# Masked graph attention, two layers: the score products in 32x64 tiles of TensorE in place of 32x128

## The chip, the cores and the metric

The kernel runs on one core of a Trainium2 chip. The metric is the device time of one execution in microseconds (us). Lower is better. Matrix products run on TensorE (PE in the profile), which first loads a stationary operand (its weights, PEld in the profile) and then streams a moving operand through the array; results land in PSUM and are read by VectorE (DVE), ScalarE (ACT)[...].

## What is computed

Sixteen graphs of 1024 nodes with 256 features each, float32, with an adjacency matrix per graph. Two layers follow each other; both have the form x + layer(relu(layernorm(x)), adj). The change lies in the first layer's attention:

```python
normed = layer_norm(x, gamma1, beta1)
qkv    = normed.reshape(b_, n_, H, HD).transpose(0, 2, 1, 3)      # H = 8 heads of HD = 32
scores = jnp.einsum('bhqd,bhkd->bhqk', qkv, qkv) * scale
masked = jnp.where(adj_matrix[:, None, :, :] > 0, scores, -jnp.inf)
attn   = jax.nn.softmax(masked, axis=-1)
out    = jnp.einsum('bhqk,bhkd->bhqd', attn, qkv)
x = x + out.transpose(0, 2, 1, 3).reshape(b_, n_, d_)
y = layer_norm(x, gamma2, beta2)
return x + gelu(y @ W1 + b1) @ W2 + b2
```

Queries, keys and values are the same array. The second layer is one graph attention head over 256 features, with logits from h a_12 h^T, leaky relu, the same mask, softmax and an output projection.

## The kernel before, in words

The program holds two versions of the computation; a small test at its start picks one, and with these inputs `fast_path` runs. All of what follows is there.

**Tiles.** For each graph `b`, `va` holds the normalized rows (128 nodes on the partitions, 256 features), and `kT` the same transposed: two groups `g` of four heads, each head on 32 partitions, 1024 nodes in the free dimension. Attention is done in 512 units, one for each graph (16), half of the queries (`qh`, 512 wide), group of four heads (`g`) and tile of 128 keys (`kt`).

**One unit.** `scores` makes the products of four heads, each with its 128 keys as the stationary operand (32 partitions by 128 columns) and its 512 queries as the moving one. Head `j` of a group uses the partitions `32 j` to `32 j + 31`, so the four products lie in four row groups of the array. They go to two PSUM tiles `sc0` and `sc1` of two heads each, a bank for a head (the name in the profile is `s`). The DVE adds the mask (L971), the ACT takes the exponential (L974), and one unit later `weigh` multiplies the result `e` with the values (L987, tile `o`): four products of 128 partitions by 32 columns, side by side in the four column groups. For graph 0 alone (`by_pe`), the mask of the first two heads is added on TensorE ahead of the score products by a product of the mask with an identity matrix.

**The rest of TensorE's work.** All other products (L570: the first layer's MLP `ph` and `po`, the second layer's `lg`, `pa`, `pg`, `pf`, `puT`) go through the helper `matmul`, which splits a product of 128 columns in four of 32 columns. Transposes are 128 by 128. Each float32 product stands in the profile as two weight loads and two matmuls: the 2048 score products of the program are 4096 records at L950. They are called its two passes below.

**Order.** The order of instructions on each engine is fixed by the program: six streams (attention, the previous graph's MLP and second layer, preparation, prologue, masks, setup) are merged by places written out by hand, with a `clock` that tells deferred pieces when they are due. The attention of one graph is interleaved with the remaining layers of the graph before it: between two units' products lie some 4 us of L570 products. At the end a dependency from each instruction to the one before it on its engine fixes the order for good.

Of the kernel before, what the change touches and what calls it, by code (L numbers as in the profile page):

```python
# [16 lines left out]
P = 128  # L17
# [476 lines left out]
def fast_path(  # L494
# [28 lines left out]
    nc = tc.nc  # L523
# [41 lines left out]
    def matmul(out, lhsT, rhs, start=True, stop=True):  # L565
        if not quarters[0]:
            nc.tensor.matmul(out, lhsT, rhs, start=start, stop=stop)  # L567
            return
        for c in range(0, P, HD):
            nc.tensor.matmul(out[c : c + HD], lhsT[:, c : c + HD], rhs, start=start, stop=stop)  # L570
# [165 lines left out]
    def defer(us, f):  # L736
        deferred.append((clock[0] + us, len(deferred), f))

        return clock[0] + us
# [145 lines left out]
    def make_turns():  # L885
        room = 3 - open_sums[0] - bool(summed) if open_sums[0] else 100
        while turns and turns[0][0] <= room:
            n, f = turns.pop(0)
            room -= n
            f()  # L890
# [40 lines left out]
    def attention(b, st):  # L931
        va, kT = st["va"], st["kT"]


        def scores(qh, g, kt):
            qs = slice(qh * QW, (qh + 1) * QW)
            sc = [
                psc.tile([P, 2, QW], F32, tag=f"sc{i}", name=f"s_{b}_{g}_{qh}_{kt}_{i}") for i in range(2)
            ]

            by_pe = 2 if b == 0 else 0
            if by_pe:
                for j in range(by_pe):
                    matmul(
                        sc[j // 2][:, j % 2, :], ident8, st[qh][:, kt // 2, :, kt % 2], start=True, stop=False
                    )
                clock[0] += 0.45
            for j in range(GH):
                r = slice(j * HD, (j + 1) * HD)
                nc.tensor.matmul(  # L950
                    sc[j // 2][:, j % 2, :],
                    kT[r, g, kt * P : (kt + 1) * P],
                    kT[r, g, qs],
                    start=j >= by_pe,
                    stop=True,
                )
            mb = st[qh][:, kt // 2, :, kt % 2].unsqueeze(1).to_broadcast([P, 2, QW])
            es = []
            if b == 0 and kt % 2:

                odd = midp.tile([P, 2, 2, QW], F32, tag="mid", name=f"odd_{g}_{qh}_{kt}")
            for i in range(2):
                if b == 0 and kt % 2:
                    e = odd[:, i]
                elif kt == 0:
                    e = accp.tile([P, 2, QW], F32, tag=f"acc{i}", name=f"acc_{b}_{g}_{qh}_{i}")
                else:
                    e = ep.tile([P, 2, QW], F32, tag="e", name=f"e_{b}_{g}_{qh}_{kt}_{i}")
                masked = sc[i]
                if 2 * i >= by_pe:  # L970
                    nc.vector.tensor_tensor(e, masked, mb, op=ALU.add)  # L971
                    masked = e
                es.append(e)
                weights = lambda e=e, masked=masked: nc.scalar.activation(e, masked, AF.Exp, scale=SCALE)  # L974
                if i == 0:
                    weights()
            return es, weights

        acc = {}


        def weigh(qh, g, kt, es):
            if kt == 0:
                acc[g, qh] = pso.tile([P, QW], F32, tag="o", name=f"o_{b}_{g}_{qh}")
            o = acc[g, qh]
            for j in range(GH):
                nc.tensor.matmul(  # L987
                    o[j * HD : (j + 1) * HD, :],
                    va[:, kt, (g * GH + j) * HD : (g * GH + j + 1) * HD],
                    es[j // 2][:, j % 2, :],  # L990
                    start=(kt == 0),
                    stop=(kt == NT - 1),
                )
            if b == 0 and kt % 2:

                if kt > 1:
                    for n, (e, w) in enumerate(zip(es, odds[g, qh])):
                        defer(1.0 + 2.5 * n, lambda e=e, w=w: nc.vector.tensor_add(e, e, w))
                odds[g, qh] = es
            if kt == NT - 1:  # L1000
                c = tmpp.tile([P, QW], F32, tag="w2", bufs=3, name=f"os_{b}_{g}_{qh}")
                nc.vector.tensor_copy(c, o)
                weighed.append((b, qh, g, c, [s[g, qh] for s in (sums, odds) if s]))

        sums, odds = {}, {}


        def add_up(qh, g, kt, e, i):
            if b == 0 and kt % 2:
                return  # L1010
            nc.gpsimd.dma_start(sums[g, qh][i], e, accum_op=ALU.add)  # L1011

        units = [(qh, g, kt) for qh in range(NQH) for g in range(NG) for kt in range(NT)]
        for u in units:
            make_turns()
            es, rest_of_weights = scores(*u)
            go_on()
            rest_of_weights()
            qh, g, kt = u
            if kt == 0:  # L1020
                sums[g, qh] = es
            else:
                for i in range(2):
                    defer(2.0 + 1.5 * i, lambda u=u, e=es[i], i=i: add_up(*u, e, i))
            scored.append((weigh, (*u, es)))
            yield

    def go_on():
        was_weighed, was_summed, was_totalled = weighed[:], summed[:], totalled[:]
        for l in (weighed, summed, totalled):  # L1030
            l.clear()
        if scored:
            f, args = scored.pop()
            f(*args)
        summed.extend(was_weighed)
        for args in was_summed:
            total(*args)
        for args in was_totalled:
            turns.append((2, lambda args=args: finish(*args)))
        clock[0] += 2.0  # L1040
# [351 lines left out]
    def stream_a():  # L1392
        for b in range(B):
            yield from spread(attention(b, states[b]), 32, b, b + 1)
        yield from spread(close_attention(), 4, B, B + .1)
# [146 lines left out]
```

## Time and profile before

| | |
|---|---|
| median of 3 runs | 3503.76 us (3500.55 to 3506.12) |
| profiled execution | 3501.46 us, of which the span is 3499.6 us |
| TensorE clock granted | 0.998 |
| PE busy | 3445.0 us (98% of the span), 46590 matmuls |
| PE weight loads | 1673.9 us, 46590 loads, beside the matmuls |
| DVE busy | 2758.3 us (79%) |
| ACT busy | 1857.8 us (53%) |
| POOL busy | 1412.8 us (40%) |
| score products (L950) | 592.5 us of PE busy time, 4096 matmuls |
| value products (L987) | 549.2 us in three groups, 4096 matmuls |

The profile comes from one execution, followed by the hardware profiler. A group of instructions is a row with the source line, the engine, the operation, the tile written and the tiles read, the shape, the count, the busy time and the mean duration of one. A duration of a matmul is its own from start to a modelled end; matmuls overlap, so the busy time of a group is far less than count times mean. A timeline row merges consecutive instructions of one group, with the start of the first and the time from it to the end of the last.

### The profile page before, as it was taken

To read this page: it belongs to the slowest core of one execution; us is meant where nothing else is said; L and a number is where in the kernel's file an instruction comes from. 1 tells how busy PE (TensorE), PEld (TensorE's weight loads), DVE (VectorE), ACT (ScalarE), POOL (GpSimd) and SP (SyncE) were. 2 spreads that over 40 slices of the span, in tenths; PEclk is the share of its full clock that TensorE was granted. 3 is DMA by queue.
4 is the path that set the end of the run, shared out by engine and by line. 5 is a ranking of instruction groups with operands and counts; after the bars stand their busy time and mean duration, and the time that the engine had idled before them with its cause. 6 is when DMAs were issued, how large, how long until landed. Compare 5 with 4: busy or idle time off the path is not lost.

```text
span 3499.6 us, 107320 instructions
## 1 busy us (share of the span) xinstructions
PE 3445.0 (98%) x46590; PEld 1673.9 (48%) x46590; DVE 2758.3 (79%) x5193; ACT 1857.8 (53%) x2184; POOL 1412.8 (40%) x1708
## 2 busy tenths in 40 slices
PE   6999999999999999999999999999999999999998
PEld 2244444444444444444444444444444444444477
DVE  6878788787877878888787888878878777887754
ACT  4555555555555555555555555555555555555522
POOL 3444443434434344343444534344344443434220
PEclk9999999999999999999999999999999999999999
DMA  7798889999899998989989899998989989899720
GB/s 183 147 182 173 181 164 185 182 186 188 161 187 176 191 184 165 181 167 190 195 167 183 165 185 185 177 190 164 186 177 191 183 165 179 171 191 182 147 63 14
DMA packets 281860, 597.81 MB, mean 171 GB/s; under 512 B 94882, under 2 KB 130084, under 8 KB 281380
## 3 DMA queue, kind: packets, MB, share of 16 engines
q0 software_dynamic: 124416, 453.04, 70.1%
q1 hardware_dynamic: 154276, 134.41, 15.5%
q8 instruction: 368, 6.03, 0.7%
q10 hardware_dynamic: 2688, 3.41, 0.3%
q14 instruction: 112, 0.92, 0.1%
HBM read 104.21 MB, written 16.78 MB: 35 GB/s over the span
## 4 chain that ended last, share of the span: by engine, by line
PE 94%; DVE 3%; DMA 1%; issue 1%; ACT 0%; POOL 0%; ACTq 0%; SPq 0%; DVEq 0%; POOLq 0%
PE s L950 15%; PE o L987 13%; PE pa L570 12%; PE po L570 12%; PE ph L570 12%; PE lg L570 10%; PE pg L570 3%; PE pf L570 3%; PE puT L570 3%; PE den L901 2%; PE ptf L1193 1%; PE pty L1117 1%; PE ptk L801 1%; PE ptos L922 1%; PE pa L567 1%
## 5 line engine op out<-in xcount | busy, mean ns | idle before, releaser
L974 ACT ACTIVATE e<-e 128x1024 f32<-128x1024 f32 x852 | 896.0, 1057 | 964.3 <-DVE e L971 728.3
L1011 POOL DMA_DIRECT2D acc<-e x864 | 754.9, 890 | 1438.3 <-DMA acc<-e 637.3
L971 DVE TENSOR_TENSOR e<-s,mk 128x1024 f32<-128x1024 f32 x852 | 1002.6, 1217 | 181.2 <-PE s L950 155.4
L950 PE MATMUL s<-kT 32*128 32x512 f32 x4096 | 592.5, 643 | 3.5 <-DVE odd L971 2.7
L987 PE MATMUL o<-e,va 128*32 128x512 f32 x3456 | 461.8, 605 | 2.1 <-ACT e L974 2.1
L570 PE MATMUL pa<-gw,e 128*32 128x258 f32 x7648 | 453.0, 380 | 0.0
L570 PE MATMUL lg<-fT,uT 128*32 128x256 f32 x7680 | 447.3, 379 | 0.0
L570 PE MATMUL ph<-yT,w 128*32 128x256 f32 x7808 | 446.5, 379 | 0.0
L570 PE MATMUL po<-w,hid 128*32 128x256 f32 x7680 | 439.3, 379 | 0.0
L570 PEld LDWEIGHTS ph<-yT,w 128*32 128x32 f32 x7808 | 255.3, 110 | 211.8 <-issue 51.1
L570 PEld LDWEIGHTS po<-w,hid 128*32 128x32 f32 x7680 | 250.3, 110 | 208.8 <-issue 58.3
L570 PEld LDWEIGHTS pa<-gw,e 128*32 128x32 f32 x7648 | 248.4, 110 | 212.0 <-issue 56.5
L570 PEld LDWEIGHTS lg<-fT,uT 128*32 128x32 f32 x7680 | 249.6, 110 | 209.0 <-issue 43.4
L1241 DVE SCALAR_TENSOR_TENSOR e<-lg,gw,mk 128x256 f32<-128x256 f32 x512 | 223.2, 477 | 72.0 <-PE lg L570 61.5
L1247 ACT ACTIVATE e<-e,shift 128x512 f32<-128x512 f32 x256 | 183.1, 717 | 181.6 <-DVE e L1246 116.0
L1144 DVE TENSOR_TENSOR hid<-ph,b1c 128x512 f32<-128x512 f32 x256 | 175.8, 687 | 91.6 <-PE ph L570 80.1
L950 PEld LDWEIGHTS s<-kT 32*128 32x128 f32 x4096 | 162.7, 184 | 163.8 <-issue 112.0
L987 PEld LDWEIGHTS o<-e,va 128*32 128x32 f32 x3456 | 68.6, 108 | 330.3 <-issue 187.3
L974 ACT ACTIVATE acc<-acc 128x1024 f32<-128x1024 f32 x124 | 131.1, 1057 | 132.9 <-DVE acc L971 128.4
L1246 DVE SCALAR_TENSOR_TENSOR e<-e 128x512 f32<-128x512 f32 x256 | 193.1, 754 | 8.8
L971 DVE TENSOR_TENSOR acc<-s,mk 128x1024 f32<-128x1024 f32 x124 | 146.1, 1218 | 20.2 <-PE s L950 19.8
L793 POOL TENSOR_TENSOR nrm<-nrm,g 128x256 f32<-128x256 f32 x128 | 112.9, 882 | 63.8 <-DVE nrm L727 63.8
(145 smaller groups left out, 3820.9 us busy)
## 6 DMA issues: line engine op xcount, KB each, us to landing
acc<-e POOLq DMA_DIRECT2D x864, 512.0 KB, 6.1
adj<-in_adj_dram SPq DMA_DIRECT2D x248, 256.0 KB, 5.6
h<-in_x_dram SPq DMA_DIRECT2D x64, 256.0 KB, 6.1
xb<-in_x_dram SPq DMA_DIRECT2D x128, 128.0 KB, 4.3
out_dram<-z SPq DMA_DIRECT2D x128, 128.0 KB, 4.0
adj<-in_adj_dram SPq DMA_DIRECT2D x4, 512.0 KB, 6.8
mk<-mq SPq DMA_TRANSPOSE x128, 6.5
w<-in_L_gnn_W_dram ACTq DMA_DIRECT2D x2, 1024.0 KB
```

What stands on the lines that cost most here:

```text
L570: nc.tensor.matmul(out[c : c + HD], lhsT[:, c : c + HD], rhs, start=start, stop=stop)
L793: nc.gpsimd.tensor_mul(nrm, nrm, g1)
L901: nc.tensor.matmul(den[j * HD : (j + 1) * HD, :], ones, acc[j // 2][:, j % 2, :], start=acc is accs[0], stop=acc is accs[-1],)
L950: nc.tensor.matmul(sc[j // 2][:, j % 2, :], kT[r, g, kt * P : (kt + 1) * P], kT[r, g, qs], start=j >= by_pe, stop=True,)
L971: nc.vector.tensor_tensor(e, masked, mb, op=ALU.add)
L974: weights = lambda e=e, masked=masked: nc.scalar.activation(e, masked, AF.Exp, scale=SCALE)
L987: nc.tensor.matmul(o[j * HD : (j + 1) * HD, :], va[:, kt, (g * GH + j) * HD : (g * GH + j + 1) * HD], es[j // 2][:, j % 2, :], start=(kt = ...
L1011: nc.gpsimd.dma_start(sums[g, qh][i], e, accum_op=ALU.add)
L1144: nc.vector.tensor_tensor(hid[:, f0 : f0 + 2, :], ph, b1c[:, f0 : f0 + 2].unsqueeze(2).to_broadcast([P, 2, CW]), op=ALU.add,)
L1241: nc.vector.scalar_tensor_tensor(e[:, j, :], lg[:, j, :], gw[:, kt, D : D + 1], st[c // 2][:, kt // 2, qs, kt % 2], op0=ALU.add, op1=ALU.add,)
L1246: nc.vector.scalar_tensor_tensor(e, e, ALPHA, e, op0=ALU.mult, op1=ALU.max)
L1247: ready = defer(2.5, lambda: nc.scalar.activation(e, e, AF.Exp, bias=shift))
```

## The change

The product of a head is split in two: its first 64 keys, then its last 64 keys, each against the same 512 queries. The stationary operand of one is 32 partitions by 64 columns, its result lies on 64 partitions of the same PSUM bank, and a unit has eight products where it had four. What reads the scores is not changed, nor is the order of anything else, and the planner's `clock` is not moved by it.

```diff
@@ scores @@
             for j in range(GH):
                 r = slice(j * HD, (j + 1) * HD)
-                nc.tensor.matmul(
-                    sc[j // 2][:, j % 2, :],
-                    kT[r, g, kt * P : (kt + 1) * P],
-                    kT[r, g, qs],
-                    start=j >= by_pe,
-                    stop=True,
-                )
+                for c in range(0, P, P // 2):
+                    nc.tensor.matmul(
+                        sc[j // 2][c : c + P // 2, j % 2, :],
+                        kT[r, g, kt * P + c : kt * P + c + P // 2],
+                        kT[r, g, qs],
+                        start=j >= by_pe,
+                        stop=True,
+                    )
```

## The prediction

> **What bounds the kernel now.** I read the shares of the engines first, then the chain that ended last, then one unit of attention in the timeline.
>
> ```profile
> PE 3445.0 (98%) x46590; PEld 1673.9 (48%) x46590; DVE 2758.3 (79%) x5193; ACT 1857.8 (53%) x2184; POOL 1412.8 (40%) x1708
> ...
> PE 94%; DVE 3%; DMA 1%; issue 1%; ACT 0%; POOL 0%; ACTq 0%; SPq 0%; DVEq 0%; POOLq 0%
> ...
> L950 PE MATMUL s<-kT 32*128 32x512 f32 x4096 | 592.5, 643 | 3.5 <-DVE odd L971 2.7
> L987 PE MATMUL o<-e,va 128*32 128x512 f32 x3456 | 461.8, 605 | 2.1 <-ACT e L974 2.1
> ...
> L950 PEld LDWEIGHTS s<-kT 32*128 32x128 f32 x4096 | 162.7, 184 | 163.8 <-issue 112.0
> L987 PEld LDWEIGHTS o<-e,va 128*32 128x32 f32 x3456 | 68.6, 108 | 330.3 <-issue 187.3
> ```
>
> TensorE is the bound: busy for 98%, 94% of the chain, and before the 4096 score matmuls idle for 3.5 us in all. By stretch, from 240 to 3300 us it idles for less than 4 us in 3060. So whatever a score unit takes on TensorE goes into the end time one to one, and a faster reader of the scores is worth nothing. "Busy" hides the loss, though: value products have the same count per unit as score products, the same 512 moving columns, and take less. The timeline of one unit shows why (start, us, engine, group, count; each line is from a window narrow enough to hold that step alone):
>
> ```profile
> 1004.21 0.40 PE L570 MATMUL ph<-yT,w 128*32 128x256 f32 x4
> ...
> 1004.54 0.20 PEld L950 LDWEIGHTS s<-kT 32*128 32x128 f32 x4 [0.41 <-DVE e L1241]
> ...
> 1004.54 0.71 PE L950 MATMUL s<-kT 32*128 32x512 f32 x4
> ...
> 1004.64 0.20 PEld L950 LDWEIGHTS s<-kT 32*128 32x128 f32 x4
> ...
> 1005.07 0.61 PE L950 MATMUL s<-kT 32*128 32x512 f32 x4
> ...
> 1005.61 0.16 PEld L987 LDWEIGHTS o<-e,va 128*32 128x32 f32 x8 [0.76 <-issue]
> ...
> 1006.06 0.61 PE L987 MATMUL o<-e,va 128*32 128x512 f32 x4
> ```
>
> Four score matmuls start together, one for each head's first pass, and 0.53 us later the four of the second pass. Between the two passes of `o` it is 0.45 us, and from the second pass of `o` to the next `ph` (first start 1006.49) 0.43. So a pass of 512 columns streams in 427 ns (2 x 213 of `ph`, whose passes of 256 columns follow each other at 215), whether it has 32 rows or 128. The rest is transition. The starts of single instructions, which the trace holds in ns, split it (they repeat in nearly all of the 512 units to within 2 ns):
>
> - `ph`'s last matmul starts 20 ns after its first and streams for 213; the score loads start 93 ns after that. This is the drain at the switch from 128x32 tiles to 32x128.
> - The first score matmul is recorded 1 ns after its load, but streams only from 107 ns later: its duration is 692 where the second pass has 587, and the loads of the second pass start 108 ns after the first ones. So 105 ns is **weight load with nothing to hide it**, because the array was drained.
> - The four starts are 7 ns apart, 20 ns from first to fourth. The last score start is followed by the load of `o` after 517 ns: 427 of streaming and 90 of drain.
> - `o`'s own first load lies bare for 25 ns (617 against 592).
>
> A unit of score and value products is thus 4 x 427 = 1708 ns of streaming and (93 + 105 + 20) + (90 + 25 + 20) = 353 ns of transition, 2.06 us, as the timeline has it.
>
> **What the Trainium skill says.** "TensorE: Matmul & The Clock Gate", section "LDWEIGHTS (loading the stationary operand)", prices a load by its columns alone, P / 1.2 ns: 107 for 128 and 27 for 32. The trace agrees with both (105 and 25). Its "Part 3: Packing small matmuls" says that row and column tiles compose and that a further tile adds about 4 ns; here a float32 tile, being two pairs of load and matmul, adds 7. The same part says that a load overlaps a running matmul only in another row group; the trace differs, since the second loads of `o` start at 1005.63, all on the same 128 rows, while its first pass streams. "TensorEngine Tiling (Array Packing)", section "Tiling Modes", lists 32x64 with eight tiles, and under "Key Properties" has a change of mode drain the engine: the 90 to 95 ns above.
>
> **The change, part by part.**
>
> 1. *Streaming.* Each pass has eight tiles of 32x64 where it had four of 32x128. If the eight run side by side, a pass stays at 427 ns. No row of before has this shape. Its neighbours do: four row tiles run together (L950), and four column tiles on the same rows run together (L987), so the same partitions can feed four streams at once; two would be asked of them. Lower bound: 0, since a pass's length comes from its 512 columns, which stay. Upper bound: the two halves of a head one after the other, 2 x 427 = 854 ns more per unit. I take 0.
> 2. *Bare weight load.* 128 columns become 64. The two measured points, 25 ns for 32 and 105 for 128, give 0.83 ns a column, so 52 for 64: a gain of **53 ns** per unit. If the halves' loads were one after the other, the gain is 0; if half as much again is gained, 80. The loads of the second pass stay hidden by the first one's 427 ns.
> 3. *Stagger.* Eight starts in place of four, 7 ns apart: the last starts 47 ns after the first, not 20. The drain to `o` counts from the last tile, so the loss is **27 ns** per unit; with the skill's 4 ns a tile it is 8 (8 x 4 - 4 - 20), with 13.5 ns a tile it eats the gain of step 2.
> 4. *Issue.* 2048 more products, 4096 more loads and 4096 more matmuls, 8192 more instructions. A unit's score part will have 16 pairs in about 1.05 us, 65 ns a pair; `ph` is fed at 8 pairs in 430 ns, 54 a pair, without a gap, so the sequencer is fast enough: 0. While the eighth tile's first pass starts, the second passes of seven others wait in the queue, 14 instructions. In graph 0's `den` (L901) each tile has four passes in a row, and its fourth tile starts while some 17 instructions of the other three wait; the starts there are 13 ns apart, so nothing stops. The instruction queue moved 6.03 MB for 93180 PE instructions, so it moves 0.53 MB more, beside a DMA share of 0.7%: 0, covered by the queue ahead of TensorE.
> 5. *Waits.* The waits for a free PSUM tile stay on the first product of heads 0 and 2, the signals on the last product of heads 1 and 3; behind them the same instructions wait. DVE's add (L971) starts 20 to 50 ns sooner, and that is slack. No DMA is added, and nothing is moved past a queue. The switches of tile shape stay as many, so 93 + 90 ns stay: the drain after 32 rows and after 128 rows differs by 3 ns, and I see no reason for columns to change it.
>
> Sum: -53 + 27 = -26 ns per unit, times 512 units = **-13.3 us**. Of these, 32 units are graph 0's, where TensorE also waits for other engines (200 us busy in the first 240); they are 0.8 us of the sum, within its error. The profiled execution took 3501.46 us (span 3499.6), 2.3 below the median; I apply the sum to the median: 3503.76 - 13.3 = 3490.5 us.
>
> **Rivals.**
>
> - *The halves of a head don't run together* (slower). Both halves want the same 32 rows' moving data at the same time with another column half, a combination that the profile doesn't show in float32. Then each pass takes two streams: 512 x (854 - 26) ns = +424 us, 3928 us. For it: 32-row and 64-column tiles were never seen together here. Against it: `o` and all of L570 read the same rows four times at once without loss. If only a share f of a stream is lost, the change turns to a loss from f = 26 / 854 = 3%: so a small clash suffices, for instance 50 ns a pass, which gives 512 x (100 - 26) ns = +38 us, 3542.
> - *The loads of the two halves are serial, the streams are not*: no gain in step 2, the stagger stays: 512 x 27 ns = +13.8 us, 3517.6. For it: one row group has to take two loads. Against it: `o`'s four loads start 7 ns apart on the same rows and lie bare for only 25 ns.
> - *The gain is larger*: the stagger is hidden or 4 ns a tile: 512 x (53 - 8) = -23 us, 3481; with all of the bare load gone, -107 + 27 = -80 ns, -41 us, 3463, which nothing speaks for.
> - *It doesn't do what it says*: if the eight products were issued in the order that makes a later tile wait behind an earlier one's second pass, a unit would have a third and a fourth pass: the first rival's number again.
>
> **How the numbers follow.** About 0.2% (7 us) is what a measurement of this kernel can tell from no change, or 14 ns per unit. The forecast, -8 to -45 ns per unit, has 0.68, with 0.06 of it short of 14 ns; serial loads or a wider stagger 0.14, half of it within 0.2%; a clash of streams, small or full, 0.16; the large gain 0.02. That makes faster 0.64, same 0.13, slower 0.23. The range goes from the largest plausible gain (-23 us, and 3 for the runs' own spread) to the serial loads (+14 and 3): 3478 to 3520; left out are the clash and the large gain.
>
> **What would show it.** Right: the score loads with 64 columns at about 130 ns (between 108 and 184), the first-pass matmuls at 639 and the second at 587, starts 47 ns apart from first to eighth, 0.48 us between the passes, and PE busy at L950 lower by 10 to 15 us with twice the count. Wrong: two starts of score matmuls more per unit at 427 ns from each other (first rival), or a first pass still at 692 (serial loads), or starts over 13 ns apart.

## The result and the profile after

The changed kernel takes 3491.76 us in the median of 7 runs (3487.36 to 3503.31), the kernel before 3503.76 in 7. The ratio is 0.9964, 95% interval 0.9952 to 0.9977: faster by 0.36%, about 12.6 us. The profiled execution took 3488.4 us, its span is 3486.6, 13.0 us less than before. The lines of the page that answer to those of before (POOL is GpSimd, which starts the accumulating DMA transfers):

```profile
PE 3432.9 (98%) x50686; PEld 1634.1 (47%) x50686; DVE 2759.6 (79%) x5193; ACT 1858.0 (53%) x2184; POOL 1415.0 (41%) x1708
...
PE 91%; DMA 3%; DVE 3%; issue 1%; ACT 0%; POOL 0%; SPq 0%; ACTq 0%; POOLq 0%; DVEq 0%
...
L952 PE MATMUL s<-kT 32*64 32x512 f32 x8192 | 579.9, 616 | 4.0 <-DVE odd L973 3.2
L989 PE MATMUL o<-e,va 128*32 128x512 f32 x3456 | 461.8, 605 | 2.1 <-ACT e L976 2.1
...
L952 PEld LDWEIGHTS s<-kT 32*64 32x64 f32 x8192 | 120.9, 130 | 164.8 <-issue 118.3
```

PE's busy time falls by 12.1 us; the score products (now L952) fall from 592.5 to 579.9, 12.6 us, with twice the count, and the main group of value products stays at 461.8 to the tenth. TensorE is still the bound, with 91% of the chain. One unit in the timeline (start, us, engine, group, count; each line is again from a window that holds one step):

```profile
1005.31 0.17 PEld L952 LDWEIGHTS s<-kT 32*64 32x64 f32 x8 [0.41 <-issue]
...
1005.31 0.69 PE L952 MATMUL s<-kT 32*64 32x512 f32 x8
...
1005.36 0.18 PEld L952 LDWEIGHTS s<-kT 32*64 32x64 f32 x8
...
1005.79 0.63 PE L952 MATMUL s<-kT 32*64 32x512 f32 x8
...
1006.35 0.16 PEld L989 LDWEIGHTS o<-acc,va 128*32 128x32 f32 x8 [0.81 <-issue]
```

All eight first-pass matmuls are under way at once, and all eight second passes follow 0.48 us later (0.53 before). The second loads start 0.05 us after the first (0.10 before): a load of the first pass lasts 128 ns where it lasted 181. In ns, as medians from the starts of single instructions in graphs 1 to 15: a first pass lasts 638 (692 before), a second 587 (587), the eight starts span 47 (four spanned 20), and 518 after the last score matmul the first value matmul starts (517). From the first score matmul to the first value matmul it is 1044 ns, not 1071: **27 ns a unit**.

The starts of units give the same over the whole run. Counted from the span's start, unit 352 begins 9.1 us earlier than before and unit 511 13.2 us earlier: 4.1 us in 159 units, 26 ns each. With every start set beside that of the same matmul in the trace before, the stretches from the first score matmul to the first value matmul are shorter by 12.7 us in graphs 1 to 15. Graph 0 gives another 1.7 us; all other intervals add up to a loss of 2.4, of which 1.8 lie in twelve single intervals that differ by over 0.25 us, some gained and some lost. Behind the last matmul 1.0 us is gained.

### The profile page after: what moved, and what is told of

It reads as the page before. It is cut to its first block, busy times and chain, and to the rows that moved or that the text cites. A ratio compares the mean times of both kernels' runs of the same rounds, so it can differ in the third digit from the quotient of the medians.

```text
span 3486.6 us, 115512 instructions
## 1 busy us (share of the span) xinstructions
PE 3432.9 (98%) x50686; PEld 1634.1 (47%) x50686; DVE 2759.6 (79%) x5193; ACT 1858.0 (53%) x2184; POOL 1415.0 (41%) x1708
## 3 DMA queue, kind: packets, MB, share of 16 engines
q1 hardware_dynamic: 154276, 134.41, 15.1%
q8 instruction: 400, 6.55, 0.8%
## 4 chain that ended last, share of the span: by engine, by line
PE 91%; DMA 3%; DVE 3%; issue 1%; ACT 0%; POOL 0%; SPq 0%; ACTq 0%; POOLq 0%; DVEq 0%
PE s L952 15%; PE o L989 13%; PE pa L570 12%; PE ph L570 11%; PE po L570 11%; PE lg L570 10%; PE pg L570 3%; PE puT L570 3%; PE pf L570 3%; DMA acc<-e 2%; PE den L901 2%; PE pty L1119 1%; PE ptf L1195 1%; PE ptk L801 1%; PE pa L567 1%
## 5 line engine op out<-in xcount | busy, mean ns | idle before, releaser
L952 PE MATMUL s<-kT 32*64 32x512 f32 x8192 | 579.9, 616 | 4.0 <-DVE odd L973 3.2
L989 PE MATMUL o<-e,va 128*32 128x512 f32 x3456 | 461.8, 605 | 2.1 <-ACT e L976 2.1
L952 PEld LDWEIGHTS s<-kT 32*64 32x64 f32 x8192 | 120.9, 130 | 164.8 <-issue 118.3
```

Of the source, the lines that this page charges most:

```text
L952: nc.tensor.matmul(sc[j // 2][c : c + P // 2, j % 2, :], kT[r, g, kt * P + c : kt * P + c + P // 2], kT[r, g, qs], start=j >= by_pe, stop= ...
L989: nc.tensor.matmul(o[j * HD : (j + 1) * HD, :], va[:, kt, (g * GH + j) * HD : (g * GH + j + 1) * HD], es[j // 2][:, j % 2, :], start=(kt = ...
```

## Experiments

The theory is that a unit costs 0.83 ns for each column of the bare load and 6.7 ns for each tile after the first, everything else staying. Its rivals are that the stagger costs nothing, that the readers' earlier start is what counts, and that tiles of one row group disturb each other. Times are medians, ratios against the kernel before run beside them. Of each edit the diff shows the loop alone: the slices below it take the width of its steps, and what else differs is said in words.

**Four tiles of 32x64, half the keys** (the load alone) and **eight of 32x32, half the keys** (shorter load, more stagger). Both leave out the products of the last 64 keys of each tile in graphs 1 to 15, whose scores are left over from graph 0, and both allocate the two score tiles once, ahead of the loop.

```diff
-                for c in range(0, P, P // 2):
+                for c in range(0, 64 if b else P, 64):     # the second kernel: steps of 32
```

> Four tiles of 32x64: for graphs 1 to 15 the second 64 keys of each tile get no product (their scores are left over in PSUM from graph 0), so the load is shortened and the stagger stays that of four tiles. The two score tiles are allocated once. Theory (a unit costs 0.83 ns a column of bare load and 6.7 ns for each further tile, the rest constant): first-pass matmul 638 ns, starts 20 ns from first to last, 480 ns between the passes; -53 ns in 480 units and -26 in the 32 of graph 0, -26 us against the kernel before. Rival (the gain comes from the readers' earlier start, not from TensorE's own time): they start some 50 ns earlier here too, but the load and stagger then don't add up to the time. Rival (stagger costs nothing): the same as the eight-tile kernel, -13 us.

> Eight tiles of 32x32 for the first 64 keys; the other 64 keys get no product in graphs 1 to 15 (left over from graph 0, which has sixteen tiles of 32x32). Score tiles allocated once. Theory: bare load 25 ns in place of 105, stagger 47 in place of 20: -80 + 27 = -53 ns in 480 units, about 0 in graph 0's 32; first-pass matmul 612 ns, 453 ns between the passes; -25 us against the kernel before. Rival (stagger costs nothing): -80 ns, -38 us. Rival (the load is not by columns below 64): -26 ns as with eight tiles of 64, -13 us.

Measured: 3484.45 us, ratio 0.9952 (0.9940 to 0.9964), and 3487.30 us, ratio 0.9953 (0.9943 to 0.9963). The groups of score matmuls, four tiles of 64 first:

```profile
L951 PE MATMUL s<-kT 32*64 32x512 f32 x4352 | 568.4, 619 | 4.4 <-DVE odd L972 3.1 <-DVE e L972 1.1
```

```profile
L951 PE MATMUL s<-kT 32*32 32x512 f32 x8704 | 569.0, 604 | 5.5 <-DVE odd L972 4.5 <-DVE e L972 1.0
```

Against 592.5 before, that is -24.1 and -23.5 us of TensorE time; the theory had -26 and -25. In both a unit lasts 1017 to 1018 ns, 53 less than before: 638 and 20 ns of stagger in the first kernel, 612 and 47 in the second. So load and stagger are two terms that add up, and both rivals on them fall: with free stagger the second kernel's TensorE time would be 38 us lower. The end times gain only 17 us of the 24; the rest is in single waits: intervals that differ by over 0.25 us from the trace before add 8.2 us in the first kernel and 7.3 in the second. Half of the score work is left out in both, and a second pass still lasts 587 ns, as with all of it in the changed kernel. So the amount of work in a pass is not what costs: **here a pass cost its 512 moving columns, whether four or eight tiles shared it**.

The control, eight tiles of 32x64 with all the keys and the score tiles allocated once (`kept_sc`, made ahead of the loop):

```diff
-            sc = [psc.tile([P, 2, QW], F32, tag=f"sc{i}", ...) for i in range(2)]
+            sc = kept_sc
```

> The changed kernel with the two score tiles allocated once, as in the two kernels with half the keys: all the work, eight tiles of 32x64. It is their control. Theory: the allocation costs nothing on TensorE, a unit stays at 1044 ns from its first score matmul to the first value matmul, -13 us against the kernel before. Rival (the allocation itself brought part of the -17 us of the two half kernels): it is faster than the changed kernel by 5 us or more.

Measured: ratio 0.9962 (0.9951 to 0.9974), 1044 ns a unit. The allocation brings nothing that the time shows.

**The loops exchanged**

```diff
-            for j in range(GH):
-                r = slice(j * HD, (j + 1) * HD)
-                for c in range(0, P, P // 2):
+            for c in range(0, P, P // 2):
+                for j in range(GH):
+                    r = slice(j * HD, (j + 1) * HD)
```

> The eight tiles of 32x64 with the loops exchanged: the first halves of the four heads, then the second halves. Score tile 0 is then complete with the sixth product in place of the fourth, and its reader can start 13 ns later. Theory (TensorE's own transitions alone count): the same as the changed kernel, -13 us against the kernel before, starts still 7 ns apart. Rival (readers' earlier start is the gain): a quarter of it lost, -10 us. Rival (neighbouring tiles of one row group hold each other up a little): starts closer than 47 ns in all, up to -10 us more.

Measured: 3491.99 us, ratio 0.9974 (0.9964 to 0.9985), that is -9 us, with an interval from -12.6 to -5.3: it holds the -10 of the second theory and only touches the changed kernel's -12.6. The trace decides better than the time: 47 ns of stagger and 1044 ns a unit, as with the halves inside. So neighbouring tiles of one row group were not seen to hold each other up. In this trace unit 352 starts 5.8 us earlier than before and unit 511 9.8 us earlier, 25 ns a unit; the few us to the changed kernel arise before unit 100. The trace answers the rival on the readers' start too: the first add of a unit on the DVE starts 1245 ns after the first score matmul (median of graphs 1 to 15), later than in the kernel before (1232) and in the changed kernel (1211), and the unit is as short. The gain does not come from the readers.

**Two heads split, two whole**

```diff
-                for c in range(0, P, P // 2):
+                w = P // 2 if j < 2 else P
+                for c in range(0, P, w):
```

> Heads 0 and 1 of a group in four tiles of 32x64, heads 2 and 3 whole in two tiles of 32x128. Theory (a change of tile shape drains the array, and tiles run together only within one shape): two streams after each other, 854 ns more, a drain of 90 and a bare load of 52 more per unit, some +1.0 us per unit, +510 us against the kernel before. Rival (tiles in different row groups run together whatever their width): starts 7 ns apart, -10 us or so.

Measured once: 3985.87 us, +479 us. The unit in the timeline (the first row runs on over both widths):

```profile
1005.06 2.15 PE L953 MATMUL s<-kT 32*64 32x512 f32 x12
```

```profile
1005.54 0.61 PE L953 MATMUL s<-kT 32*64 32x512 f32 x4
```

```profile
1006.08 0.70 PE L953 MATMUL s<-kT 32*128 32x512 f32 x2
```

The two whole heads start only 0.54 us after the second pass of the split ones, 427 of streaming, 20 of stagger and some 90 of drain, and with a bare load of their own. A unit lasts 2075 ns, 1004 more than before, where the steps of the prediction give 1003. The time is 35 us short of 512 x 1.004. Of these, 15 lie in graph 0, where part of it fills waits (after 32 units the kernel is 17 us behind, not 32), and some 10 in later waits that it fills; the rest was not followed up. So here a change of width drains just as a change of rows does, and a split of some heads only is a large loss.

**Sixteen tiles of 32x32**

```diff
-                for c in range(0, P, P // 2):
+                for c in range(0, P, 32):
```

> All the work, in sixteen tiles of 32x32. Theory: bare load 25 ns (-80), stagger 15 x 6.7 = 101 ns (+81): the two cancel, +1 ns per unit, 0 us against the kernel before (within 5 us). Rival (stagger costs nothing): -80 ns, -41 us. Rival (the queue ahead of TensorE holds too little: behind the sixteenth tile's first pass 30 instructions wait): the last tiles start a pass late, +427 to +854 ns per unit, +219 to +437 us.

Measured: 3518.49 us, ratio 1.0052 (1.0039 to 1.0065), +18 us: none of the three. Yet inside the unit the theory holds: 612 ns, 100 ns of stagger, 1071 from the first score to the first value matmul, as before, and 592.5 us of TensorE time, as before. The loss lies behind it. The first value matmuls of a unit, and the second ones, with sixteen tiles:

```profile
1004.60 0.65 PE L989 MATMUL o<-e,va 128*32 128x512 f32 x4
```

```profile
1005.05 0.63 PE L989 MATMUL o<-e,va 128*32 128x512 f32 x4
```

and the first ones in the kernel before:

```profile
1005.61 0.64 PE L987 MATMUL o<-e,va 128*32 128x512 f32 x4
```

The four start at 0, 7, 22 and 38 ns, not at 0, 7, 13 and 20. Since each column tile then goes on at its own pace, pass after pass, the fourth is still 17 ns late when the next transpose or score product waits for the array to drain: over the switches from 160 to 3300 us the stagger of the last four is 39 ns in the mean, where it was 22. At 17 ns, 512 units make 8.7 us; start by start, the trace of graphs 1 to 15 shows 7.9 us lost there. I had costed the wait of 30 instructions at nothing or at a whole pass; it was neither. Most of the other half of the 18 us is in waits: 22 single intervals that differ by over 0.25 us from the trace before add 8.4 us.

**Twelve tiles of 32x32, three quarters of the keys**, to see when the stagger widens. The products of the last 32 keys are left out in graphs 1 to 15, and the score tiles are allocated once.

```diff
-                for c in range(0, P, P // 2):
+                for c in range(0, 96 if b else P, 32):
```

> Twelve tiles of 32x32: the first 96 keys of each tile; the last 32 keys get no product in graphs 1 to 15 (left over from graph 0, which has sixteen tiles). Score tiles allocated once. Theory of the two terms: -80 of load, 11 x 6.7 - 20 = +54 of stagger, -26 ns in 480 units, -13 us against the kernel before. What is open is why with sixteen tiles the four value products after the scores start 38 ns apart from first to last in place of 20, which is then paid again at the next change of shape. If their instructions were still outside the queue[...], then here 24 pairs of scores and 8 of the value products just fit: 20 ns, and -13 us. If the sequencer falls behind in proportion to the pairs it issues: some 29 ns, and -9 us.

Measured: 3508.30 us, ratio 1.0014 (1.0001 to 1.0028). On the question asked the trace answers: `o` starts within 20 ns in the median, the unit lasts 1044 ns, and the score products take 581.2 us, -11.3. So the stagger widens between 24 and 32 pairs of score instructions; what changes there was not measured. But the time missed by 18 us: in this trace graph 0 loses 9.0 us against the kernel before, and single intervals that differ by over 0.25 us lose another 7.3 behind it, more than the 11 us saved.

**Graph 0 apart from the others.** Three runs ask where such waits come from.

```diff
-                for c in range(0, P, P // 2):
+                w = 64 if b == 0 else 32
+                for c in range(0, P, w):
```

> Graph 0 in eight tiles of 32x64, graphs 1 to 15 in sixteen of 32x32; all the work. With sixteen tiles everywhere 18 ns a unit (some 9 us) were seen in the trace, as the value products' wider stagger paid at the next change of shape; another 8 us lay in single long waits, two thirds of them from graph 0 to 1. Theory A (graph 0, where TensorE waits for other engines and masks, can't take sixteen tiles): the 8 us go, +9 us against the kernel before. Theory B (the long waits come from the number of instructions in the later graphs): they stay, +17 us. In both the steady slope is +18 ns a unit.

The second kernel has the two widths exchanged. The third has twelve tiles of 32 in graphs 1 to 15, where it leaves out the last 32 keys, and eight of 64 in graph 0, and allocates the score tiles once.

> Graph 0 in sixteen tiles of 32x32, graphs 1 to 15 in eight of 32x64; all the work. Theory A (graph 0): half to all of the 8 us come back, -5 to -9 us against the kernel before. Theory B (the later graphs' instructions): -13 us, as the changed kernel. In both the steady slope is -26 ns a unit.

> Twelve tiles of 32x32 (the first 96 keys; the last 32 get no product, their scores are left over) in graphs 1 to 15, graph 0 in eight tiles of 32x64 with all its keys. With sixteen tiles in graph 0, twelve came out at +5 us where the steady slope of -26 ns a unit would give -13. In all four traces with sixteen tiles in graph 0 its last unit starts 3 to 4 us later, in none of the others. Theory A (graph 0): that goes, and some 4 us or more with it, 0 us or faster against the kernel before. Theory B (single waits in the later graphs, with more instructions): +5 us as before.

Measured: ratios 1.0030 (1.0022 to 1.0038), +11 us; 0.9968 (0.9952 to 0.9984), -11 us; and 1.0009 (0.9997 to 1.0021), +3 us. The first is near theory A, and its interval leaves B out; the second lies between, and the third nearer to B, but their intervals hold both. The traces show a share for graph 0: its last unit starts 3 to 4 us later, against the unit before it, in all four kernels that have sixteen tiles there, and in none of the six with eight. Four units on, 1.5 to 1.9 us of that are made up again. They also show waits in the later graphs that A can't explain. TensorE's waits in the third kernel, whole span (who waited for whom, us in all, times, longest):

```profile
PE den L902 <- DMA acc<-e: 9.6, 5, 3.2
```

and in the changed kernel:

```profile
PE den L901 <- DMA acc<-e: 2.1, 2, 1.2
```

`den` sums what the accumulating DMA has added up, and that queue is late more often there. From 240 to 3300 us TensorE idles for 15.1 us in the third kernel and for 4.4 in the changed one. These are single executions; the control with eight tiles and the same allocation idles for 7.1 us, so the allocation or chance may have a part in it. All of them have a unit of 1044 ns, so the pace alone is not the cause. Nor do the waits simply add up: graph 0 costs 9.0 us in the first trace with twelve tiles and gains 2.3 in the one with eight tiles there, yet both spans are 6 us above the span before, as the later single intervals lose 15.7 us in place of 7.3. More instructions to fetch (the instruction queue moves 7.05 MB in the third kernel, 6.55 in the changed one), the left-over scores, or DMA engines that are busy for 0.92 to 0.93 of the time from 160 to 3300 us with either count of tiles might be the cause, and no run separates them. **This stays open.** No version was found that beats the changed kernel with all the work done: by the measured terms, tiles of 128, 64 and 32 columns cost 105 + 20, 52 + 47 and 25 + 100 ns, and 64 is the least of the three.

## Why the prediction was right

- *What bounds.* Right. TensorE's own time fell by 12.1 us, the span by 13.0, the median by some 12.
- *Streaming at 0.* Right, and it was the step with the widest bounds. Eight tiles of 32x64 run together; a second pass lasts 587 ns as before, and so it does in every other arrangement that was tried. The first rival, two streams per pass, would have shown two more groups of starts.
- *Bare load, -53.* Right: 638 in place of 692, 54 ns. The prediction's interpolation between 32 and 128 columns hit 64, and 32 columns on 32 rows gave 612, 25 over the second pass, as `o` has it on 128 rows. So the bare load went by columns alone, as the Trainium skill has it in "TensorE: Matmul & The Clock Gate", section "LDWEIGHTS (loading the stationary operand)": its formula gives an estimate of 53 ns for 64 columns, and 51 were measured (638 - 587). The rival of serial loads falls: both halves' loads last 128 ns in the first pass, and they start 7 ns apart.
- *Stagger, +27.* Right: 47 in place of 20. The 4 ns a tile in "Part 3: Packing small matmuls" of that page are too few for float32 here, where 6.7 were measured from four to sixteen tiles. The prediction's margin is too wide, though: seven steps less the 20 ns of before reach the 53 of the load at 10.4 ns a tile, not at 13.5.
- *Issue at 0.* Right for eight tiles, and still for twelve, where `o` starts within 20 ns. The instruction queue's 0.52 MB more were as worked out. The argument from `den`, that a queue with some 17 waiting instructions doesn't stop, did not carry to sixteen tiles, where the tiles behind the scores start up to 18 ns later.
- *Waits at 0.* Right in the changed kernel, within 1 us: idle time from 240 to 3300 us went from 3.4 to 4.4. That this slack is thin, the prediction didn't see: the kernels with twelve tiles lose their whole gain to waits.
- *The sum.* -13.3 us against -13.0 in the span and -12.0 between the two medians. The mechanism carries 12.7 us of it; that the rest comes out within 1 us is partly luck, since graph 0 and the single waits happened to cancel, and executions of the changed kernel alone spread over 16 us.

## What to carry to other kernels

When a kernel that TensorE bounds changes tile shape in short groups, look at the first group after each change: a matmul that lasts longer than its followers showed here a weight load that nothing hid, and its excess went with the columns of the load (105, 51 and 25 ns for 128, 64 and 32). Splitting the columns shortened that load; it pays as long as all tiles of the group get the same shape and the stagger of the added tiles, which the next change of shape waits for, costs less. And follow a stagger beyond its group: here column tiles kept their own pace until the next drain.

## What the runs showed of the hardware that was not expected

- Column tiles that start late stay late: 38 ns at the first value products were still 36 ns forty-four matmuls and 2.8 us later (medians of the sixteen-tile kernel; 20 and 20 in the kernel before).
- A change of width alone, from 64 to 128 columns with 32 rows each, drained the array like any other: 0.54 us from the start of the last pass to the next start, some 90 ns of it drain. The wider tiles lay in other row groups, and waited all the same.
- The drain did not depend on the shape left: 517 to 518 ns from the last score matmul to the first value matmul with 128, 64 and 32 columns alike.
